# Source scores of layer 0 by GpSimd products and ScalarE sums, and a later place for some small GpSimd operations of layer 1

## The chip, the cores and the metric

The kernel runs on one core of a Trainium2 chip. The metric is the device time of one execution in microseconds (us). The core has a matrix engine (TensorE, PE in the profile; its weight loads are a row of their own, PEld), three engines for elementwise work (VectorE or DVE, ScalarE or ACT, GpSimd or POOL) and a queue engine (SyncE or SP) that issues transfers. The engines run side by side. Each takes its own instructions strictly in order and waits on semaphores for the others.

## The reference, cut to what matters

There are 3327 nodes with 256 features each, and a sparse 0/1 adjacency matrix with about four neighbours in a row. Two layers follow each other, each with a residual and a layer norm around it.

```python
# layer 0
Wh = h @ W
src = Wh @ a[:F_out]                 # one number per node
dst = Wh @ a[F_out:]
e = leaky_relu(src + dst.T, 0.2)
att = softmax(where(adj > 0, e, NEG_INF), axis=1)
h_prime = att @ Wh
...                                  # a GRU cell of h_prime and h
x = layernorm(x + gru)
# layer 1, two steps n = 0, 1; S is adj, R is (adj + I) by row sums
A  = top_p_attention(Xa, W1, W2, W3) # softmax row cut to its 0.9 nucleus, renormalised
Xf = R @ Xf
Xa = A @ Xa
Z  = Z + Xf @ U1[n].T + Xa @ U2[n].T
# after both steps
h = layernorm(X + Z) * ln_g + ln_b
x = layernorm(x + h)
```

The cut keeps, in a row of sorted probabilities, those whose preceding sum is below 0.9. Probabilities equal to the last one kept are ties, and how many of them stay depends on the order of their indices.

## The kernel before, in words

**Tiles and stages.** The 3327 rows make 26 tiles of 128 rows (the last has 127). In the profiled execution layer 0 lies from 0 to some 400 us, step 0 of layer 1 from there to about 930 us, and step 1 from there to the end. The orders of PE, ACT, DVE and POOL are written out by hand: each engine runs its instructions in the order in which the program text issues them. There is no planner.

**Start of layer 0** (`Layer0.run`). `weights()` makes two things out of W and the vector a: `by_a`, W times both halves of a laid along partitions (narrow PE products L813 and ACT copies L817), and `by_row`, W times the second half, repeated on all partitions (L822 to L824). Then tile groups are turned (`turn`, PE transposes and an ACT copy) and the destination scores are taken from x and `by_row` on DVE (`scores`, L855). The source scores come from PE: `project` (L872) multiplies the transposed tile by a column of `by_a`, 128x1 products, and ACT copies them to `ds` (L876).

**Loop of layer 0.** It runs in phases, six for each tile. In each phase DVE searches a part of an adjacency tile for its ones (`neighbours`, L935), and one to five tiles that are under way each go one step further in `tile(t)`: counts and offsets on ACT (`over1` L972 and after, `mid` L986, `tell` L988, `y` L990), a PE product that brings every edge its row's data (`pe` L1000), ACT's copies (`ei` L1004, `erow` L1005), DVE's choice of neighbour (`which` L1009 to `k` L1017), five gathers by POOL (L667), the weights and sums, and the GRU. `project` is called once before the loop for tiles 0 and 1 and once in each of the phases 3 to 26. `tell_src` (DVE, four small operations) splits source scores into the three parts that `pe` carries, at phases 1, 10 and 28 for tiles 0-1, 2-7 and 8-25. In phase 4 ACT issues the loads of the GRU's weights (L1217). From phase 13 on `gates_weights` multiplies them by W (PE L833, copies L838 on DVE and ACT), and at phases 8 and 10 `make_weights` prepares layer 1's weights (DVE copies L656 and L661).

**Step 1 of layer 1** (`Layer1.run`, the loop L2412 to L2481). Work item i of step 1 handles one tile of rows. Its stages are spread over several turns of the loop:

- three items ahead: logits (PE L1762) and the copy of them by ACT (L1765);
- two items ahead: the largest eight of each part of a row (DVE MAX8 L1778), the row's maximum, the exponentials (ACT L1860, and of the candidates L1872);
- one item ahead: a sorted list of the largest values (`list_1`), and `list_2`, which calls `settle` (L1802): DVE finds the threshold t and the number d of ties to drop, and POOL works out `lim` (L1822), `short` (L1824), `many` (L1826) and the flag (L1827) that tells whether the list was long enough. `gone` (POOL L1944 and L1945) lists the ties to drop. `mask` needs it: a match-replace over the whole row (DVE L1954, 3327 wide) drops these ties, and a whole-row product with a sum (L1924) keeps what is at least t;
- in the item's own turn: PE transposes the masked row block in seven groups (`turn` L2042, ACT copies L2044) and multiplies by the values (`times`, `pav` L2058). `one_over` (POOL L1933 and L1934) inverts the row sum to `rA`;
- after it: ACT scales the product by `rA` (`scaled`, L2066), POOL adds the neighbour term (L2067), and two layer norms follow in `tile_end` and `by_sums`. Each norm calls `sums`: an ACT sum (L2014), the negated mean `min` on POOL (L2016), an ACT sum of squares with that bias (L2019), three small POOL operations for scale and shift `mv` (L2021 to L2023), an ACT application (L2025). Between the norms POOL multiplies by `ln_g` (L2089) and adds x plus bias (L2091).

Two norms run at once: the second norm of an older tile (tags `bt`) and the first of a newer one (`at`). `propagate` computes R times the values from POOL's gathers (L667): PE L1983, ACT L1987, POOL add L1988. `put_aside_1` and `put_aside_2` store rows whose flag is set in a list of hard tiles: a flag cast on POOL (L2110), the PE product `pos` (L2113), small POOL operations (L2117 to L2127), an index on DVE (L2144) and POOL's `left_over` scatter (L2145). The hard tiles are treated again, with other methods, at the end.

**The order around the change.** `product(i, slots)` runs through the item's seven groups of PE work, and behind group g it calls the functions in `slots[g]`, in the order of their entry. That order decides where each engine's instructions stand. On POOL, one turn of the loop reads before the change: `left_over`, two gathers, `far` to `pay`, add L2067, the two `min` L2016, three gathers, `one_over`, `lim`, `short`, `many`, flag, `gone`, the six `mv`, add L1988, flag cast, product L2089, add L2091.

Of the kernel before, what the change touches and what calls it, by code (L numbers as in the profile page):

```python
# [16 lines left out]
P = 128  # L17
N = 3327
D = 256
# [694 lines left out]
class Layer0:  # L714
# [6 lines left out]
    def __init__(self, sh, ctx, adj, W, WT, a, wihT, whhT, b_ih, b_hh):  # L721
# [8 lines left out]
        self.by_a = keep.tile([P, DC, 2], F32, name="by_a")  # L730
        self.by_row = keep.tile([P, D], F32, name="by_row")
# [75 lines left out]
    def weights(self):  # L807

        nc = self.nc
        for c in range(DC):  # L810
            pa = self.ps.tile([P, 512], F32, tag="sm", name=f"pa{c}")
            for o in range(DC):
                nc.tensor.matmul(  # L813
                    pa[:, 0:2], self.WT_sb[:, o, c * P : (c + 1) * P], self.a_sb[:, o::DC],
                    start=(o == 0), stop=(o == DC - 1),
                )
            nc.scalar.copy(self.by_a[:, c, :], pa[:, 0:2])  # L817

        pr = self.ps.tile([P, 512], F32, tag="sm", name="pr")
        for o in range(DC):  # L820
            ab = self.work.tile([P, 2 * D], F32, tag="rz", name=f"ab{o}")[:, :P]
            nc.vector.tensor_scalar(ab, self.sh.ones, self.a_sb[:, DC + o : DC + o + 1], None, ALU.mult)  # L822
            nc.tensor.matmul(pr[:, :D], ab, self.WT_sb[:, o, :], start=(o == 0), stop=(o == DC - 1))
        nc.vector.tensor_copy(self.by_row, pr[:, :D])  # L824
# [24 lines left out]
    def scores(self, t0, t1):  # L849

        nc, sh = self.nc, self.sh
        for t in range(t0, t1):
            r = rows(t)
            junk = self.work.tile([P, 2 * D], F32, tag="rz", name=f"junk{t}")
            nc.vector.scalar_tensor_tensor(  # L855
                junk[:r, :D], sh.x1[:r, t, :], 1.0, self.by_row[:r], ALU.mult, ALU.mult,
                accum_out=sh.x1w[:r, t, self.DST : self.DST + 1],
            )
        if t1 < NT:
            nc.sync.dma_start(  # L860
                sh.whx[t0 * P : t1 * P, :].rearrange("(t p) w -> p t w", p=P), sh.x1w[:, t0:t1, :]
            )
        else:
            move_rows(nc.sync, sh.whx[t0 * P : N, :], sh.x1w[:r, t0, :], r)

    def project(self, t0, t1):

        nc, r = self.nc, rows(t1 - 1)
        pw = self.ps.tile([P, 512], F32, tag="sm", name=f"pw{t0}")[:, : t1 - t0]
        for t in range(t0, t1):  # L870
            for c in range(DC):
                nc.tensor.matmul(  # L872
                    pw[:r, t - t0 : t - t0 + 1], self.xT[:, c, cols(t)], self.by_a[:, c, 0:1],
                    start=(c == 0), stop=(c == DC - 1),
                )
        nc.scalar.copy(self.ds[:r, t0:t1], pw[:r])  # L876
# [270 lines left out]
    def run(self):  # L1147
# [38 lines left out]
        with self.tc.manual_schedule(engines=engines):  # L1186
# [13 lines left out]
            self.project(0, 2)  # L1200
            for _ in range(5):
                find()
            while phase < EVERY * NT or tiles:
                advance(FINDS[phase % EVERY])
                if phase == 1:
                    self.tell_src(0, 2)
                if 2 < phase <= NT:
                    self.project(phase - 1, phase)
                if phase == 10:
                    self.tell_src(2, 8)  # L1210
                if phase == NT + 2:
                    self.tell_src(8, NT)
                if phase in (8, 10):
                    next(qk_weights)
                if phase == LOAD_AT:
                    for w, src in ((self.plain, wih), (self.whh, whh)):
                        nc.scalar.dma_start(w, src.rearrange("(c p) d -> p c d", p=P))  # L1217
                if phase > 2 * EVERY:
                    next(gates, None)
# [19 lines left out]
class Layer1:  # L1239
# [562 lines left out]
    def settle(self, lst, before, last, thr2, r, drop, flag, tag, room=None):  # L1802
# [16 lines left out]
        )  # L1819
        lim = self.small("lim8", f"lim8{tag}")  # L1820
# [7 lines left out]
        return t, d, lim  # L1828
# [74 lines left out]
    def list_2(self, i):  # L1903

        nc, v = self.nc, self.items[i]
        n, r, tag = v.n, v.r, v.tag
        length = LIST[1]
        e = v.e[:r, :length]
        before = self.work.tile([P, length], F32, tag="before", name=f"before{tag}")
        nc.vector.tensor_tensor_scan(before[:r], e, e, 0.0, ALU.add, ALU.add)  # L1910
        v.t, v.d, v.lim = self.settle(
            v.lst, before[:r], v.last, v.thr2, r, DROP, self.flag[:r, n, v.at : v.at + 1], tag
        )

# [94 lines left out]
    def sums(self, h, r, tag):  # L2009
# [6 lines left out]
        nc.gpsimd.tensor_scalar(minus[:r], s[:r], -1.0 / D, None, ALU.mult)  # L2016
# [247 lines left out]
    def hard(self, k):  # L2264
# [20 lines left out]
        t, d, _ = self.settle(lst, before, last, thr2, P, HARD_DROP, flag, tag, room)  # L2285
# [98 lines left out]
    def run(self):  # L2384
# [5 lines left out]
        with self.tc.manual_schedule(engines=engines | {mybir.EngineType.Pool}):  # L2390
# [17 lines left out]
            self.gone(NT)  # L2408
            self.mask(NT)
# [3 lines left out]
            for i in range(NT, total):  # L2413
# [11 lines left out]
                slot(1, self.one_over, i)  # L2425
# [5 lines left out]
                if i + 1 < total:  # L2431
                    self.list_1(i + 1)
                    slot(1, self.list_2, i + 1)
                    slot(1, self.gone, i + 1)
                if i + 2 < total:
# [24 lines left out]
                for g in (0, 1, 2):  # L2460
                    slot(g, next, older, None)
# [136 lines left out]
```

## Time and profile before

| what | before |
|---|---|
| median of 3 runs | 1696.85 us (1692.40 to 1698.18) |
| profiled execution, its own time | 1693.33 us |
| its span | 1691.3 us |
| mean granted TensorE clock | 0.932 |
| POOL L667, gathers of layer 0, 130 | 1.04 us each |
| DVE L935, searches, 104 | 1.03 us each |
| POOL L2091, 26 adds | 3.58 us each |
| PE L2058, 1352 products | 0.40 us each |

A group line of the page names the source line, the engine, the operation, the output and input tiles, the count, the busy time, the mean in ns, and the idle time ahead of the group. A timeline line has the start and duration in us, the engine, the line, the operation, and in brackets the idle time ahead of it with what ended it. A wait line reads: engine, the tile and line that waited, what it waited for, then total us, how many times, the longest. A stretch line gives the stretch and its length, then for PE, its weight loads, DVE, ACT and POOL the busy time with the number of instructions, then the granted PE clock, the DMA share and GB/s.

### The profile page before, as it was taken

How to read it: one execution, taken by the hardware profiler on the slowest of the kernel's cores; microseconds unless marked ns; L12 is line 12 of the kernel's file. 1: busy time of each engine (PE TensorE's matmuls, PEld its weight loads, DVE VectorE, ACT ScalarE, POOL GpSimd, SP SyncE). 2: the span in 40 equal slices, each digit the busy share in tenths (PEclk: the TensorE clock that was granted, in tenths of full speed). 3: DMA queues.
4: the chain of work that ended last, by engine and by line, in shares of the span. 5: the costliest groups of instructions: out<-in, count | busy, mean ns of one | idle time of the engine just before them, and what ended most of it. 6: DMA issues, size and time to landing. Idle time of an engine off the chain costs nothing.

```text
span 1691.3 us, 27502 instructions
## 1 busy us (share of the span) xinstructions
PE 1457.9 (86%) x7899; PEld 980.9 (58%) x7899; DVE 1348.6 (80%) x4847; ACT 1080.6 (64%) x2631; POOL 1062.3 (63%) x1577
## 2 busy tenths in 40 slices
PE   4899999876999999999988799999999999875524
PEld 3766666544555555555554477776776666664413
DVE  5799999438877888887862999999998987875992
ACT  4478888646677777777753566666665676763511
POOL 0466666415566666666663468888888787778431
PEclk7599999987999999999999899999999999997766
DMA  8977775223344444434442112222222222211000
GB/s 256 332 261 257 256 256 131 75 79 95 102 116 110 111 123 113 109 109 114 115 119 58 35 54 72 68 57 72 67 68 70 64 63 63 60 53 33 19 6 5
DMA packets 101639, 178.75 MB, mean 106 GB/s; under 512 B 25977, under 2 KB 64119, under 8 KB 101479
## 3 DMA queue, kind: packets, MB, share of 16 engines
q0 software_dynamic: 26288, 73.68, 17.1%
q1 hardware_dynamic: 61818, 93.49, 17.0%
q10 hardware_dynamic: 13372, 9.74, 1.8%
q8 instruction: 65, 1.06, 0.3%
q14 instruction: 96, 0.78, 0.2%
HBM read 139.86 MB, written 37.06 MB: 105 GB/s over the span
## 4 chain that ended last, share of the span: by engine, by line
PE 41%; DVE 17%; POOL 14%; ACT 11%; issue 11%; DMA 6%; POOLq 0%; ACTq 0%; DVEq 0%; SPq 0%
PE pav L2058 11%; PE pl L1762 5%; POOL g L667 4%; DVE at L935 4%; DMA g<-x1k,uidx 3%; PE pav L1659 3%; PE pt L2042 3%; PE pxf L1983 2%; PE pc L1422 2%; POOL g L1598 2%; ACT at L2044 2%; PE pxf L1402 2%; PE plt L1634 2%; ACT p L1860 1%; ACT array L1765 1%
## 5 line engine op out<-in xcount | busy, mean ns | idle before, releaser
L2058 PE MATMUL pav<-xu,at 128*128 128x256 f32 (+2 forms) x1352 | 346.1, 399 | 35.6 <-ACT at L2044 35.6
L2058 PEld LDWEIGHTS pav<-xu,at 128*128 128x128 f32 (+2 forms) x1352 | 249.2, 195 | 135.0 <-ACT at L2044 63.3
L1778 DVE MAX8 cand<-array 128x8 f32<-128x104 f32 (+5 forms) x1233 | 260.3, 287 | 8.5 <-ACT array L1765 8.1
L1765 ACT COPY array<-pl 128x416 f32<-128x416 f32 (+3 forms) x402 | 184.5, 512 | 129.2 <-PE pl L1762 128.9
L1762 PE MATMUL pl<-kT,qT 64*128 64x416 f32 (+3 forms) x804 | 205.6, 569 | 8.7 <-ACT array L1765 7.6
L667 POOL DMA_INDIRECT g<-y_rows,edge x130 | 140.0, 1077 | 46.2 <-issue 33.8
L667 POOL DMA_INDIRECT g<-whx,edge x130 | 135.0, 1039 | 47.0 <-issue 37.3
L667 POOL DMA_INDIRECT g<-x_rows,edge x130 | 134.8, 1037 | 45.5 <-issue 30.8
L2044 ACT COPY at<-pt 128x512 f32<-128x512 f32 (+2 forms) x182 | 95.5, 543 | 99.6 <-PE pt L2042 99.4
L1598 POOL DMA_INDIRECT g<-x1k,uidx x130 | 136.4, 1049 | 34.5 <-issue 30.1
L1762 PEld LDWEIGHTS pl<-kT,qT 64*128 64x128 f32 (+1 forms) x804 | 67.2, 188 | 77.3 <-issue 56.8
L935 DVE FIND_INDEX8 at<-ones,array 128x8 uint32<-128x840 f32 (+1 forms) x104 | 105.9, 1027 | 0.0
L1698 POOL TENSOR_TENSOR x<-x,c 128x256 f32<-128x256 f32 (+1 forms) x26 | 26.8, 1032 | 109.5 <-ACT c L1693 109.5
L2091 POOL TENSOR_TENSOR h<-h 128x256 f32<-128x256 f32 (+1 forms) x26 | 93.2, 3584 | 2.0
L1666 DVE TENSOR_SCALAR rA<-pav 128x1 f32<-128x1 f32 (+1 forms) x26 | 4.1, 158 | 77.3 <-PE pav L1659 77.3
L1659 PE MATMUL pav<-g,w 128*128 128x257 f32 (+1 forms) x260 | 62.6, 388 | 3.4 <-DVE w L1653 3.4
L1052 PE MATMUL acc<-g,m 128*128 128x258 f32 (+1 forms) x260 | 63.2, 391 | 0.0
L1052 PEld LDWEIGHTS acc<-g,m 128*128 128x128 f32 (+1 forms) x260 | 50.7, 195 | 18.4 <-issue 7.7
L1983 PE MATMUL pxf<-g,m 128*128 128x256 f32 (+1 forms) x260 | 61.3, 383 | 0.0
L1079 PE MATMUL prz<-wih,hT 128*128 128x512 f32 (+1 forms) x104 | 51.8, 622 | 3.0 <-ACT hT L1072 1.1
L1659 PEld LDWEIGHTS pav<-g,w 128*128 128x128 f32 (+1 forms) x260 | 48.3, 193 | 10.4 <-DVE w L1653 3.8
L1886 DVE SCALAR_TENSOR_TENSOR cand<-ec,high 128x256 f32<-128x256 f32 (+1 forms) x104 | 51.4, 494 | 2.8
(556 smaller groups left out, 3830.0 us busy)
## 6 DMA issues: line engine op xcount, KB each, us to landing
array<-in_adj_dram SPq DMA_DIRECT2D x25, 1248.0 KB
array<-in_adj_dram SPq DMA_DIRECT2D x25, 415.5 KB
members<-m SPq DMA_DIRECT2D x26, 320.0 KB
m<-members SPq DMA_DIRECT2D x26, 320.0 KB
x_rows<-x ACTq DMA_DIRECT2D x25, 128.0 KB
x1k<-x ACTq DMA_DIRECT2D x25, 128.0 KB
xb_rows<-xb SPq DMA_DIRECT2D x25, 128.0 KB
y_rows<-y SPq DMA_DIRECT2D x25, 128.0 KB
```

The lines of the kernel that those rows point to most:

```text
L667: self.nc.gpsimd.indirect_dma_start(out=dst[:, b, :], out_offset=None, in_=table[:, :], in_offset=bass.IndirectOffsetOnAxis(ap=self.edge[: ...
L935: nc.vector.max_index(at[:r, g, :], self.ones8[:r], ad[:r, g, :])
L1052: nc.tensor.matmul(acc[:r, : self.WH], m[:, :r], g[:, k, :], start=(k == 0), stop=(k == EB - 1))
L1598: nc.gpsimd.indirect_dma_start(out=v.g2[:, b, :], out_offset=None, in_=sh.x1k[:, :], in_offset=bass.IndirectOffsetOnAxis(ap=v.idx[:, b : b ...
L1659: nc.tensor.matmul(v.acc[:r, : D + 1], v.w[:, b, :r], v.g2[:, b, : D + 1], start=(b == 0), stop=(b == UB - 1))
L1762: nc.tensor.matmul(pl[:r, :w], q[on], self.sh.kT[on, n, s : s + w], start=True, stop=True)
L1765: nc.scalar.copy(l[:r, h * HALF + s : h * HALF + s + w], pl[:r, :w])
L1778: self.nc.vector.max(cand[:r, g * 8 : g * 8 + 8], src[:r, g * group : min(N, (g + 1) * group)])
L1983: nc.tensor.matmul(acc[:r, :D], v.m[:, b, :r], v.g[:, b, :], start=(b == 0), stop=False)
L2044: nc.scalar.copy(at[:, :full, :r], pt[:, :full, :r])
L2058: nc.tensor.matmul(v.acc[: v.r, :D], at[:k, j - 4 * g, : v.r], V[:k, j, :], start=(j == 0), stop=(j == NT - 1))
L2091: nc.gpsimd.tensor_tensor(h, h, term, ALU.add)
```

## The change

In layer 0, `by_a` and `project` go. `by_row` now holds W times both halves of a, made by four pairs of a DVE operation and a PE product in one PSUM tile, and one copy. The source score of a tile is a product of x and `by_row` on POOL (`source_1`) and a sum over the row on ACT (`source_2`). The products of tiles 0 and 1 are issued ahead of the loop, and those of two further tiles in each of the phases 1 to 12; the sums stand at the head of the next phase on ACT. The tiles of products have two buffers. `tell_src` moves to phases 2, 8 and 15 (tiles 0-1, 2-11, 12-25), and `make_weights` to phases 18 and 20.

In step 1 of layer 1, `settle` becomes a generator that stops once t and d are known. Its last four operations run when `told` is called: at the head of slot 2 instead of inside `list_2` in slot 1 (for the last item right behind `gone`). `one_over` moves from the head of slot 1 to slot 2. The negated mean is computed by ACT. POOL's turn then reads: `left_over`, two gathers, `far` to `pay`, add L2067, three gathers, `gone`, the six `mv`, `lim`, `short`, `many`, flag, add L1988, flag cast, `one_over`, product L2089, add L2091.

```diff
-        self.by_a = keep.tile([P, DC, 2], F32, name="by_a")
-        self.by_row = keep.tile([P, D], F32, name="by_row")
+        self.by_row = keep.tile([P, 2, D], F32, name="by_row")
...
     def weights(self):
-        for c in range(DC):
-            pa = self.ps.tile([P, 512], F32, tag="sm", name=f"pa{c}")
+        pr = self.ps.tile([P, 2, D], F32, tag="sm", name="pr")
+        for k in (1, 0):
             for o in range(DC):
-                nc.tensor.matmul(
-                    pa[:, 0:2], self.WT_sb[:, o, c * P : (c + 1) * P], self.a_sb[:, o::DC],
-                    start=(o == 0), stop=(o == DC - 1),
-                )
-            nc.scalar.copy(self.by_a[:, c, :], pa[:, 0:2])
-
-        pr = self.ps.tile([P, 512], F32, tag="sm", name="pr")
-        for o in range(DC):
-            ab = self.work.tile([P, 2 * D], F32, tag="rz", name=f"ab{o}")[:, :P]
-            nc.vector.tensor_scalar(ab, self.sh.ones, self.a_sb[:, DC + o : DC + o + 1], None, ALU.mult)
-            nc.tensor.matmul(pr[:, :D], ab, self.WT_sb[:, o, :], start=(o == 0), stop=(o == DC - 1))
-        nc.vector.tensor_copy(self.by_row, pr[:, :D])
+                ab = self.work.tile([P, 2 * D], F32, tag="rz", name=f"ab{k}_{o}")[:, :P]
+                nc.vector.tensor_scalar(ab, self.sh.ones, self.a_sb[:, k * DC + o : k * DC + o + 1], None, ALU.mult)
+                nc.tensor.matmul(pr[:, k, :], ab, self.WT_sb[:, o, :], start=(o == 0), stop=(o == DC - 1))
+        nc.vector.tensor_copy(self.by_row, pr)
...
-    def project(self, t0, t1):
-
-        nc, r = self.nc, rows(t1 - 1)
-        pw = self.ps.tile([P, 512], F32, tag="sm", name=f"pw{t0}")[:, : t1 - t0]
-        for t in range(t0, t1):
-            for c in range(DC):
-                nc.tensor.matmul(
-                    pw[:r, t - t0 : t - t0 + 1], self.xT[:, c, cols(t)], self.by_a[:, c, 0:1],
-                    start=(c == 0), stop=(c == DC - 1),
-                )
-        nc.scalar.copy(self.ds[:r, t0:t1], pw[:r])
+    def source_1(self, t):
+
+        r = rows(t)
+        self.times_a[t] = m = self.work.tile([P, D], F32, tag="h", name=f"times_a{t}")
+        self.nc.gpsimd.tensor_tensor(m[:r], self.sh.x1[:r, t, :], self.by_row[:r, 0, :], ALU.mult)
+
+    def source_2(self, t):
+
+        r, m = rows(t), self.times_a.pop(t)
+        self.nc.scalar.activation(m[:r], m[:r], AF.Identity, accum_out=self.ds[:r, t : t + 1])
...
-            self.project(0, 2)
+            self.times_a = {}
+            self.source_1(0)
+            self.source_1(1)
...
-                if phase == 1:
+                for t in list(self.times_a):
+                    self.source_2(t)
+                if phase == 2:
                     self.tell_src(0, 2)
-                if 2 < phase <= NT:
-                    self.project(phase - 1, phase)
-                if phase == 10:
-                    self.tell_src(2, 8)
-                if phase == NT + 2:
-                    self.tell_src(8, NT)
-                if phase in (8, 10):
+                for t in (2 * phase, 2 * phase + 1):
+                    if t < NT:
+                        self.source_1(t)
+                if phase == 8:
+                    self.tell_src(2, 12)
+                if phase == NT // 2 + 2:
+                    self.tell_src(12, NT)
+                if phase in (18, 20):
                     next(qk_weights)
...
     def settle(self, lst, before, last, thr2, r, drop, flag, tag, room=None):
...
+        yield t, d
         lim = self.small("lim8", f"lim8{tag}")
...
-        return t, d, lim
+        yield lim
...
-        v.t, v.d, v.lim = self.settle(
+        v.settled = self.settle(
             v.lst, before[:r], v.last, v.thr2, r, DROP, self.flag[:r, n, v.at : v.at + 1], tag
         )
+        v.t, v.d = next(v.settled)
+
+    def told(self, i):
+        v = self.items[i]
+        v.lim = next(v.settled)
...
     def sums(self, h, r, tag):
...
-        nc.gpsimd.tensor_scalar(minus[:r], s[:r], -1.0 / D, None, ALU.mult)
+        nc.scalar.activation(minus[:r], s[:r], AF.Copy, scale=-1.0 / D)
...
             self.gone(NT)
+            self.told(NT)
             self.mask(NT)
...
-                slot(1, self.one_over, i)
                 slot(1, next, beside, None)
...
                     slot(1, self.gone, i + 1)
+                    if i + 2 == total:
+                        slot(1, self.told, i + 1)
...
                 for g in (0, 1, 2):
+                    if g == 2:
+                        slot(g, self.one_over, i)
+                    if g == 2 and i + 2 < total:
+                        slots[g].insert(0, lambda i=i: self.told(i + 1))
                     slot(g, next, older, None)
                     slot(g, next, last, None)
```

## The prediction

> **What bounds the kernel now.** I read the busy shares first, then busy time by stretch, then the waits of a stretch, and last the timeline of one period. The page:
>
> ```profile
> span 1691.3 us, 27502 instructions
> PE 1457.9 (86%) x7899; PEld 980.9 (58%) x7899; DVE 1348.6 (80%) x4847; ACT 1080.6 (64%) x2631; POOL 1062.3 (63%) x1577
> L2091 POOL TENSOR_TENSOR h<-h 128x256 f32<-128x256 f32 (+1 forms) x26 | 93.2, 3584 | 2.0
> ```
>
> No engine is full over the run. Step 1 of layer 1, the only part of layer 1 that is edited, runs from about 943 to 1691 us. By stretch (time, then busy time of each engine, PE clock last):
>
> ```profile
> 1043.00:1246.00 203.00, 195.05 (x972) 143.38 (x972) 188.97 (x640) 130.95 (x298) 168.30 (x289) 1.00 0.24 68
> 1381.00:1482.00 101.00, 89.99 (x433) 65.79 (x432) 84.03 (x284) 68.94 (x147) 76.44 (x137) 0.97 0.21 61
> 1482.00:1545.00 63.00, 48.59 (x232) 39.99 (x230) 44.79 (x117) 38.37 (x74) 51.36 (x96) 0.89 0.16 46
> ```
>
> In the steady stretch PE (96%) and DVE (93%) both lack only a little, so a shorter wait pays only until one of them is full. Later both have more air. The waits of the steady stretch (nine periods), total, count, longest:
>
> ```profile
> ACT h L2025 <- POOL mvbt L2023: 10.6, 9, 1.2
> PE pav L2058 <- ACT at L2044: 8.2, 18, 0.6
> DVE p L1954 <- POOL gone L1945: 4.1, 5, 0.8
> DVE array L1954 <- POOL gone L1945: 3.3, 4, 0.8
> ```
>
> All three engines stop once a period for a POOL result, or for ACT that stood waiting for POOL. One period on POOL and DVE:
>
> ```profile
> 1138.29 0.22 POOL L2016 TENSOR_SCALAR minbt<-sbt 128x1 f32<-128x1 f32 x1
> 1138.94 0.21 POOL L2016 TENSOR_SCALAR minat<-sat 128x1 f32<-128x1 f32 x1 [0.43 <-ACT junkat L2014]
> 1143.56 0.30 POOL L1933 TENSOR_SCALAR rA<-pay,sA 128x1 f32<-128x1 f32 x1
> 1144.53 0.29 POOL L1822 TENSOR_SCALAR lim<-last,e 128x1 f32<-128x1 f32 x1
> 1145.96 0.35 POOL L1944 TENSOR_SCALAR gone<-col,d 128x8 f32<-128x8 f32 x1
> 1146.40 0.34 POOL L1945 TENSOR_SCALAR gone<-gone,t 128x8 f32<-128x8 f32 x1
> 1150.71 4.06 POOL L2091 TENSOR_TENSOR h<-h 128x256 f32<-128x256 f32 x1
> ```
>
> ```profile
> 1146.77 0.09 DVE L1954 MATCH_VALUE_LOAD p<-gone,p 128x8 f32 x1 [0.82 <-POOL gone L1945]
> 1146.85 3.61 DVE L1954 MATCH_REPLACE8 p<-gone,p 128x3327 f32<-128x3327 f32 x1
> 1150.50 3.68 DVE L1924 SCALAR_TENSOR_TENSOR p<-p,t 128x3327 f32<-128x3327 f32 x1
> ```
>
> The loop that sets the 22.58 us period (1124.19, 1146.77, 1169.35) closes over POOL and DVE: `gone` releases the match-replace, the full-row product behind it (L1924) ends at 1154.18, the POOL add L2091, alone 0.72 us, is held until 0.59 us after that (4.06 us), and from there POOL works its list through, almost without a gap, to the next `gone`. That list lasts 15.17 us (22.58 less the 7.41 of the two DVE passes).
>
> **The change, step 1 of layer 1.** Three pieces leave POOL's list ahead of `gone`: the minus of the mean, 1138.31 to 1139.15 with its wait on ACT, 0.84 us; the two `one_over` operations, 1143.56 to 1144.53, 0.97; `lim`, `short`, `many` and `flag`, 1144.53 to 1145.96, 1.43. Together 3.24 us, and the list from L2091 to `gone` falls to 11.93. DVE's stall is only 0.82, so `gone` ceases to be last. What is late next: DVE's own work, 22.58 - 0.82 = 21.76, or PE's, 22.58 - 0.33 - 0.58 (its two stalls behind ACT copies L2044, which follow ACT's waits of 1.18 and 0.59 for `mvbt` and `mvat`; these come 3.24 us earlier too) = 21.67. So at most 0.8 to 0.9 a period.
>
> The postponed work is not gone. After `mvbt` and `mvat` (2.34 us behind `gone`) now come the four list operations, 1.43, and then the add L1988, 0.73, the flag cast, `one_over`, 0.97, the product L2089 and the add L2091. L1988 thus starts 3.77 us after `gone`; the product L1924 starts 3.73 after the match-replace. What POOL has not begun by then stands until it ends: L2091 4.06 for 0.72, and small POOL operations caught there last 3.3 to 3.5 us for 0.2 (L2016, L2124). Three cases. (1) `one_over` done in time: L2089 is held, L2091 ends 0.7 later than now, 8.7 us after the match-replace, and with 11.93 POOL needs 20.7 a period. (2) `one_over` held: 7.41 + 0.97 + 0.73 + 0.72 = 9.9, POOL 21.8. (3) L1988 held: 8.0 + 0.15 + 0.97 + 0.73 + 0.72 = 10.6, POOL 22.5, less the 0.57 that the first gather waits for PE today, 21.9; but `rA` is ready 9.1 after the match-replace, and ACT's L2066 wants it at 8.2 (1154.98). Behind that stand the copies L2044 of 1155.33, and PE's second stall grows from 0.58 to about 1.5. Gains of (1), (2), (3): 0.8, 0.7, about 0.1. As POOL has slack in (1), starts in it, and drifts towards (3) only as the held work eats the slack, I take 0.5 a period, ends 0 and 0.9.
>
> For ACT the minus is two 128x1 operations a period, 0.2 to 0.3 each (its 128x1 rows), beside idle time of 0.5 to 2.9 in the same period. No wait is added for POOL; ACT's Square no longer crosses to POOL and back.
>
> The Trainium skill, "SBUF — State Buffer", section "SBUF: two separate sides", says that VectorE and GpSimd share a port pair as an exclusive lock, and that a VectorE operation with two SBUF inputs shuts a reading GpSimd operation out for its whole length. The rows of L2091 agree (4.06 against 0.72, while L1988 keeps 0.73 beside the match-replace). Taken alone the rule speaks against pushing 2.4 us of POOL work towards L1924: by it case (3) is the lasting one and the steady stretch gains about 1 us instead of 6.
>
> Sum over the 26 items, by the starts of the match-replaces on DVE's timeline and the wait ahead of each. 1011 to 1282: 12 periods x 0.5 = 6 (0 to 11). 1282 to 1331: `gone` waits 4.25 and 0.99, PE follows closely: 2 (0 to 4). 1331 to 1381: periods of 25.1 that PE fills (stalls 0.3 and 0.6): 0.8 (0 to 2). 1381 to 1482: waits 3.78, 4.48, 3.83, 2.13, and PE stalls 2.24 each behind ACT: 5 of 14 (2 to 8). 1482 to 1545: periods of 28 and 17 with DVE stalled 6.30 for `gone`, POOL the busiest engine: 4 of the 4.4 by which `gone` advances (2 to 6). 1545 to 1691: DVE chain of the last tiles, not edited: 0. Together -17.8 (-4 to -31).
>
> **The change, layer 0.** Up to 34.3 us `weights()` has four pairs of ab and product in place of two pairs and four narrow products: two small DVE operations more, four PE products fewer: 0 (-0.3 to +0.3). After that PE loses 104 matmuls of some 0.35 us (a tile 0.87 to 1.03), POOL gets 26 products (0.65 to 0.73 alone, L2067, L1988; 1.03 in row L1698) and ACT 26 sums (0.51, as L2014) for 25 copies of 0.16. ACT is in order, so what is queued behind the sums matters: the weights' loads L1217, issued at 42.95 and 43.70, now wait for eight tiles' sums. With two product buffers POOL and ACT alternate at about 0.83 us a tile, so the loads go at about 45. `ei` L1004 (53.55) stands behind 24 sums and comes at about 60.4. Who waits:
>
> ```profile
> 58.30 0.69 DVE L838 COPY wih<-pm 128x512 f32<-128x512 f32 x1 [3.55 <-PE pm L833]
> 58.91 0.16 DVE L1009 TENSOR_TENSOR which<-place,ei 128x5 f32<-128x5 f32 x1
> 61.89 0.69 DVE L838 COPY wih<-pm 128x512 f32<-128x512 f32 x1 [1.54 <-PE pm L833]
> ```
>
> L1009 goes from 58.91 to about 60.6. The stalls ahead of L838 (3.55, 1.54) cover part: PE reaches the products earlier without its small matmuls. DVE's next searches start about 1.2 later (62.5 to 63.7), but all `tell_src` is then done (1.1 us, now at 79) and the weight copies moved to phases 18 and 20 (0.7) are still to come. From 73 to about 246 us DVE works without a gap, so the shift stays: +0.6 (-2 to +6, the upper end with products of 1.03 and no cover).
>
> The Trainium skill, "TensorE: Matmul & The Clock Gate", Part 1, says PE runs at half clock until it has been busy for some microseconds. The granted clock from 40 to 60 us is 0.50 to 0.60; by the rule, removing the small matmuls could keep it at half for the L833 products, which would cost about 1.8 us (first 3.7, second 1.96). I don't count it.
>
> Total -17.8 + 0.6 = -17.2. The profiled execution took 1693.33 (span 1691.3 and 2.0 around it), which gives 1676; it is 3.5 below the median of the three runs, 1696.85, from which it would be 1680. I say 1678, from the middle of the two, 1695, as I do for the rivals.
>
> **Rivals.** *Half the gain*: case (3) holds in the steady stretch, or the ACT passes of the last tiles keep PE late after 1381. For: the 0.04 us between 3.77 and 3.73. Against: POOL begins with 3.24 us of slack. 1 + 1 + 0.5 + 3 + 2 for the five stretches, less 0.6 = -7: 1688. *No change*: PE, at 96%, fills the period as soon as it is let, and layer 0 takes the late gain (+4): within 5 us, 1690 to 1700. For: waits come back elsewhere. Against: PE's own stalls are from the same POOL list. *Slower*: `rA` is late. If L1988 is held in most items (`gone` ending less than 0.1 us ahead of the match-replace is the point from which it decides), `rA` comes 0.9 us after ACT needs it, the copies L2044 and the two exp passes slip, and both PE and DVE wait about 0.6 more than today: 20 items x 0.6 = +12, and the late gain is eaten by the same delay: 1708. Against: a longer period gives POOL back its slack, so the delay corrects itself. *Layer 0 slow*: products of 1.03 as in row L1698 and nothing that covers: +6 in place of +0.6, -17.8 + 6 = -12, 1683. For: VectorE is busy beside them. Against: its rows there are mostly single-input searches L935.
>
> **How the numbers follow.** Full gain (-12 to -28) 0.48, more than that 0.05, half gain or a slow layer 0 (-5 to -12) 0.22, no change 0.11, slower 0.14. A measurement can tell 0.3%, about 5 us, from no change. So faster 0.75, same 0.11, slower 0.14. The range from 1665 to 1699 leaves about 0.05 below and 0.15 above; the likeliest case alone has 1668 to 1686.
>
> **What would show it.** Right: the DVE waits for `gone`, 43.4 us over the whole span (27.6 with `array`, 15.8 with `p` as the tile), fall below 12; ACT's L2025 waits for `mvbt` vanish; the match-replaces come 21.8 to 22.3 apart; the held 4 us moves from L2091 to L2089; the first `which` (L1009 today) comes at about 60.6. Wrong: new ACT waits for `rA` ahead of L2066, PE waits for `pos` on the flag cast, or `one_over` rows of 3 us mean that the postponed list fell under L1924; the source sums taking more than 0.9 us a tile mean a slow layer 0.

## The result and the profile after

The changed kernel takes 1674.37 us in the median of 5 runs (1668.83 to 1678.08), the kernel before 1697.11 us in the median of 5 (1692.40 to 1698.18). The ratio is 0.9867 with a 95% interval of 0.9842 to 0.9891: 22.7 us faster. The prediction said 1678 (1665 to 1699). The profiled execution took 1668.83 us with a span of 1667.0, so it is 5.5 us below the median of its kernel, as the one before was 3.8 below its own.

The page of the kernel after, the same lines as shown of before:

```profile
span 1667.0 us, 27301 instructions
PE 1427.8 (86%) x7791; PEld 956.5 (57%) x7791; DVE 1362.3 (82%) x4849; ACT 1100.7 (66%) x2710; POOL 1068.9 (64%) x1549
```

The steady stretch of step 1, again by stretch (time, busy time of PE, its weight loads, DVE, ACT, POOL, then the clock):

```profile
1043.00:1246.00 203.00, 198.61 (x995) 148.09 (x994) 196.29 (x672) 137.03 (x322) 167.71 (x276) 1.00 0.25 72
```

DVE's share of it rose from 188.97 to 196.29 us: almost full. The waits of the same stretch:

```profile
POOL mvbt L2022 <- ACT junkbt L2020: 8.1, 10, 1.6
ACT junkat L2015 <- POOL h L2068: 2.9, 9, 0.3
PE pav L2059 <- ACT at L2045: 2.6, 9, 0.3
```

No wait of DVE for `gone` is left there, none of ACT for `mvbt`, and PE's wait for the copies fell from 8.2 to 2.6. POOL still waits for ACT, but at `mvbt`, which now stands behind `gone`. One period on POOL:

```profile
1134.22 0.33 POOL L1946 TENSOR_SCALAR gone<-gone,t 128x8 f32<-128x8 f32 x1
1135.25 0.19 POOL L2022 TENSOR_SCALAR mvbt<-sqbt 128x1 f32<-128x1 f32 x1 [0.71 <-ACT junkbt L2020]
1138.62 0.29 POOL L1823 TENSOR_SCALAR flag<-many,short 128x1 f32<-128x1 f32 x1
1140.25 0.57 POOL L1935 TENSOR_TENSOR rA<-rA,minus_one 128x1 f32<-128x1 f32 x1
1140.79 0.73 POOL L2090 TENSOR_TENSOR h<-h,ln_g 128x256 f32<-128x256 f32 x1
1141.60 3.99 POOL L2092 TENSOR_TENSOR h<-h 128x256 f32<-128x256 f32 x1
```

And on DVE, where the match-replace starts without a wait:

```profile
1137.37 0.08 DVE L1955 MATCH_VALUE_LOAD p<-gone,p 128x8 f32 x1
1137.44 3.61 DVE L1955 MATCH_REPLACE8 p<-gone,p 128x3327 f32<-128x3327 f32 x1
1141.08 3.92 DVE L1925 SCALAR_TENSOR_TENSOR p<-p,t 128x3327 f32<-128x3327 f32 x1
```

`gone` is done at 1134.55, 2.8 us ahead of the match-replace. All that was postponed ends before DVE's product; the add L2092 is held under it as before (3.99 us). Over the whole span DVE waits 5.4 us for `gone`, where it waited 43.4 before. The period is 21.9 us (1115.47, 1137.37, 1159.34) in place of 22.58.

Where the time went, by the starts of the match-replaces (before, after, what the piece gained):

| piece | before | after | gain |
|---|---|---|---|
| start to the first match-replace (layer 0, step 0) | 943.54 | 938.21 | 5.3 |
| first to fourth | 67.8 | 66.8 | 0.9 |
| 12 steady periods | 270.9 | 264.0 | 6.9 |
| next 2 (waits 4.25 and 0.99) | 48.8 | 45.9 | 2.9 |
| next 2 | 50.2 | 46.7 | 3.5 |
| next 4 | 101.2 | 95.0 | 6.1 |
| last 2 | 45.1 | 43.7 | 1.4 |
| last match-replace to the end | 163.9 | 166.6 | -2.7 |

### The profile page after: what moved, and what is told of

Same layout as the page of the kernel before. It is cut to its first block, busy times and chain, and to the rows that moved or that the text cites. A ratio compares the mean times of both kernels' runs of the same rounds, so it can differ in the third digit from the quotient of the medians.

```text
span 1667.0 us, 27301 instructions
## 1 busy us (share of the span) xinstructions
PE 1427.8 (86%) x7791; PEld 956.5 (57%) x7791; DVE 1362.3 (82%) x4849; ACT 1100.7 (66%) x2710; POOL 1068.9 (64%) x1549
## 3 DMA queue, kind: packets, MB, share of 16 engines
q8 instruction: 64, 1.05, 0.3%
## 4 chain that ended last, share of the span: by engine, by line
PE 48%; DVE 16%; POOL 13%; issue 10%; ACT 7%; DMA 4%; ACTq 0%; POOLq 0%; DVEq 0%; SPq 0%
PE pav L2059 16%; PE pl L1757 6%; POOL g L667 4%; DVE at L925 4%; PE pt L2043 3%; PE pxf L1984 3%; DMA g<-x1k,uidx 3%; POOL g L1593 2%; PE pav L1654 2%; PE pc L1417 2%; PE pxf L1397 2%; PE plt L1629 1%; DVE array L1961 1%; PE pu L1569 1%; ACT array L1504 1%
## 5 line engine op out<-in xcount | busy, mean ns | idle before, releaser
L2059 PE MATMUL pav<-xu,at 128*128 128x256 f32 (+2 forms) x1352 | 339.4, 396 | 21.9 <-ACT at L2045 21.9
L1042 PEld LDWEIGHTS acc<-g,m 128*128 128x128 f32 (+1 forms) x260 | 50.5, 195 | 22.3 <-issue 7.7
L1882 DVE SCALAR_TENSOR_TENSOR cand<-ec,high 128x256 f32<-128x256 f32 (+1 forms) x104 | 56.4, 543 | 2.8
L2092 POOL TENSOR_TENSOR h<-h 128x256 f32<-128x256 f32 (+1 forms) x26 | 55.3, 2129 | 2.0
```

The lines of the kernel that those rows point to most:

```text
L1042: nc.tensor.matmul(acc[:r, : self.WH], m[:, :r], g[:, k, :], start=(k == 0), stop=(k == EB - 1))
L1882: nc.vector.scalar_tensor_tensor(v.cand[:r], ec[:r], high[:r, j : j + 1], ec[:r], ALU.is_ge, ALU.mult, accum_out=above[:r, j : j + 1])
L2059: nc.tensor.matmul(v.acc[: v.r, :D], at[:k, j - 4 * g, : v.r], V[:k, j, :], start=(j == 0), stop=(j == NT - 1))
```

## Experiments: each part alone

Layer 0 and step 1 apart, and each of the three pieces of step 1 alone.

**Layer 0 alone**: the hunks of `weights`, `source_1`, `source_2` and the loop of layer 0 as in the diff of the change, and nothing of layer 1.

```diff
-            self.project(0, 2)
+            self.times_a = {}
+            self.source_1(0)
+            self.source_1(1)
```

> Only the part of layer 0 is changed. Theory A (from the trace after: DVE's first search 1.3 us later, search 17 3.5 later, search 78 2.4 later, and nothing that gives it back): the run is 1 to 3 us slower than before, ratio 1.0006 to 1.002, with the searches as late as in the trace after. Theory B (the first match-replace of step 1 came 5.3 us earlier after the change, because layer 0 passes on less PE work): 3 to 6 us faster, ratio 0.9965 to 0.998, and the first match-replace of step 1 near 938 us. Theory C: what is late in layer 0 is absorbed by waits behind 290 us: 0, within 1 us.

Measured: 1689.78 us against 1693.73, ratio 0.9968 (0.9950 to 0.9986). **Step 1 alone**: the hunks from `settle` on, and nothing of layer 0.

```diff
-        return t, d, lim
+        yield lim
...
-                slot(1, self.one_over, i)
```

> Only the part of step 1 is changed. Theory A: the whole gain is here, 22 to 26 us, ratio 0.985 to 0.987, at least as fast as the whole change; match-replaces 21.9 us apart in the steady stretch. Theory B: 17 to 19 us, ratio 0.989 to 0.990, as layer 0 brought 5 of the 23.

Measured: 1675.81 us, ratio 0.9898 (0.9878 to 0.9919). So theory B holds for both: the layer 0 of the change is worth 2 to 8 us by the interval of its ratio, and is not a loss. **The negated mean alone:**

```diff
-        nc.gpsimd.tensor_scalar(minus[:r], s[:r], -1.0 / D, None, ALU.mult)
+        nc.scalar.activation(minus[:r], s[:r], AF.Copy, scale=-1.0 / D)
```

> Only the negated mean goes to ACT: 0.84 of the 3.24 us leave POOL's list ahead of the mask. Theory A (the list need only fall by DVE's stall of 0.8; what is beyond that pays only in the last items): steady periods of 22.58 fall to 21.95 to 22.0, 7 us, and each of the nine late waits by up to 0.84, 5 to 7 us: 12 to 14 us faster, ratio 0.992 to 0.993. Rival B (the gain goes with the work that leaves the list): 0.84 / 3.24 of 21.6 us, 5.6 us, ratio 0.9967. Rival C (ACT is as near its limit as DVE and pays for two more operations): no change, steady period 22.5 or more.

Measured: 1669.57 us, ratio 0.9864 (0.9844 to 0.9884). One line brings the whole of the gain, more than even theory A gave it. The steady period is 21.7, and of the nine late waits for `gone` three are left, 1.37, 1.53 and 1.49 us. **The four list operations alone**: `settle` as a generator and `told` as in the change, with `one_over` and the negated mean as before.

```diff
+                    if g == 2 and i + 2 < total:
+                        slots[g].insert(0, lambda i=i: self.told(i + 1))
                     slot(g, next, older, None)
```

> Only the four list operations are postponed behind the list of ties and the mv operations: 1.43 of the 3.24 us leave POOL's list ahead of the mask, and the add in front of the flag cast starts later by as much. Theory A: steady periods of 21.9 to 22.0 (7 us), late waits down by up to 1.4 each (8 to 11): 15 to 18 us faster, ratio 0.9895 to 0.991. Rival B (in proportion): 9.5 us, ratio 0.9944. Rival C (the add or the flag cast is caught under the whole-row product of DVE, as the start of the add is 3.77 us behind the list of ties and the product 3.73 behind the match-replace): the steady period stays above 22.3, the gain is under 8 us, and the add L1988 of before shows rows of 4 us.

Measured: 1690.56 us, ratio 0.9978 (0.9962 to 0.9994). Rival C comes nearest, though it is the flag cast and not the add that is caught. POOL of this kernel, one period:

```profile
1177.85 0.29 POOL L1828 TENSOR_SCALAR flag<-many,short 128x1 f32<-128x1 f32 x1
1178.10 0.64 POOL L1994 TENSOR_TENSOR h<-h,x 128x256 f32<-128x256 f32 x1
1178.68 3.58 POOL L2116 CAST flag<-flag 128x1 bf16<-128x1 f32 x1
1182.23 0.72 POOL L2095 TENSOR_TENSOR h<-h,ln_g 128x256 f32<-128x256 f32 x1
1183.03 0.79 POOL L2097 TENSOR_TENSOR h<-h 128x256 f32<-128x256 f32 x1
```

The match-replace began at 1174.46. The 1.43 us taken from the front of `gone` pushed the flag cast under DVE's product (3.58 us for 0.19), so that L2095 and L2097, 1.5 us, are both done behind the product. Before, L2089 was done ahead of it, and L2091 ended 0.59 us behind it. What that costs is seen on DVE, in the same period:

```profile
1178.18 4.04 DVE L1930 SCALAR_TENSOR_TENSOR array<-array,t 128x3327 f32<-128x3327 f32 x1
1182.56 0.67 DVE L1887 SCALAR_TENSOR_TENSOR cand<-ec,high 128x256 f32<-128x256 f32 x1
1183.28 0.82 DVE L1887 SCALAR_TENSOR_TENSOR cand<-ec,high 128x256 f32<-128x256 f32 x1
```

The last two in the kernel before, behind the product of 3.68 us:

```profile
1154.53 0.52 DVE L1886 SCALAR_TENSOR_TENSOR cand<-ec,high 128x256 f32<-128x256 f32 x1
1155.10 0.48 DVE L1886 SCALAR_TENSOR_TENSOR cand<-ec,high 128x256 f32<-128x256 f32 x1
```

DVE hardly waits for `gone` any more: in the twelve steady periods 2.35 us once and at most 0.45 otherwise. But its product, which starts beside POOL's add L1994, and the two operations beside L2095 and L2097 are together 0.85 us longer, as much as the wait of 0.82 that is gone. The period is 22.3 to 22.7, in two of the twelve 24.77 and 23.54 (in the longer one `left_over` waits 2.62 us for DVE): nothing won there. **`one_over` alone**:

```diff
-                slot(1, self.one_over, i)
...
                 for g in (0, 1, 2):
+                    if g == 2:
+                        slot(g, self.one_over, i)
                     slot(g, next, older, None)
```

> Only the inverse of the row sum is moved; POOL still waits for ACT's sums. Theory A (with that wait in place POOL is late, so the moved pair is caught under DVE's whole-row product, as the flag cast was with the list operations alone, and comes back on POOL's list): steady period 22.3 or more, ratio 0.997 to 1.004. Rival B (0.97 us off the list pays like 0.84 off it by the negated mean): period 21.7 to 21.9, ratio 0.986 to 0.990.

Measured: 1688.69 us, ratio 0.9971 (0.9958 to 0.9984), steady period 22.3, one of the twelve 24.77 with the same wait of `left_over`. Theory A, with another operation caught than it named: `rA` gets through, and the product L2089 is held.

```profile
1175.52 0.56 POOL L1934 TENSOR_TENSOR rA<-rA,minus_one 128x1 f32<-128x1 f32 x1
1176.05 3.88 POOL L2089 TENSOR_TENSOR h<-h,ln_g 128x256 f32<-128x256 f32 x1
1180.00 0.79 POOL L2091 TENSOR_TENSOR h<-h 128x256 f32<-128x256 f32 x1
```

Outside the long period DVE's wait for `gone` falls from 0.82 to between 0.10 and 0.24 us, and of what that gives 0.34 is lost again in one of DVE's operations, beside L2091 (0.82 us for 0.48).

The parts give 0.22%, 0.29% and 1.36%; the three together 1.02% (0.81 to 1.22). They don't add, and the largest is the one with the least work in it.

## Experiments: is it POOL's work or POOL's wait

The negated mean is 0.43 us of work in two operations, and a wait of 0.43 us for ACT's sum. Two kernels take these apart. Both have the negated mean on ACT and a spare operation on POOL in the old place, whose output nothing reads. The first reads a constant, the second ACT's sum:

```diff
+        spare = self.st.tile([P, 1], F32, tag="spare" + tag[0], name=f"spare{tag}", bufs=2)
+        nc.gpsimd.tensor_scalar(spare[:r], self.power[:r], -1.0 / D, None, ALU.mult)   # first kernel
+        nc.gpsimd.tensor_scalar(spare[:r], s[:r], -1.0 / D, None, ALU.mult)            # second kernel
```

> As the negated mean on ACT, but POOL still does an operation of the same kind and size in the same place, on a constant: its work is back, its wait for ACT's sum is not. The result of it is used by nothing. Theory A (what POOL lost was the wait for ACT, 0.43 in the steady stretch and up to 3.2 in the last items, not the 0.4 of work): 17 to 22 us faster, ratio 0.987 to 0.990, late waits of the match-replace for the list of ties as with the negated mean alone. Rival B (the work): half of the 0.84 is back, steady period 22.2 or more, gain 8 to 12, ratio 0.993 to 0.995.

> As the one before, but the spare operation on POOL reads ACT's sum: POOL's work and its wait are both back, while ACT still makes the negated mean for itself. Theory A (POOL's wait in the queue ahead of the list of ties is the cost): time and waits of before, ratio 0.997 to 1.000, steady period 22.5. Rival C (the gain is on ACT, whose sum of squares no longer waits for POOL): ratio 0.986 to 0.989, as with the negated mean alone.

Measured: with the work and no wait 1670.89 us, ratio 0.9860 (0.9831 to 0.9890); with work and wait 1695.43 us, ratio 1.0016 (0.9996 to 1.0036). Theory A in both. The waits of the kernel whose spare operation reads the sum, in the steady stretch:

```profile
ACT h L2027 <- POOL mvbt L2025: 10.6, 9, 1.2
PE pav L2060 <- ACT at L2046: 8.3, 18, 0.6
DVE p L1954 <- POOL gone L1945: 4.2, 5, 0.8
POOL spareat L2018 <- ACT junkat L2014: 3.9, 9, 0.4
DVE array L1954 <- POOL gone L1945: 3.4, 4, 0.9
```

They are the waits of before, to a tenth. The kernel with the constant has none of them but

```profile
PE pav L2060 <- ACT at L2046: 2.6, 9, 0.3
```

So the 0.43 us for which POOL stood behind ACT set the period, and what ACT gains by making its own bias is worth nothing by itself. How 0.43 us can bring 0.87 a period was not tried; the traces show it in the operation of POOL which the product catches. In the kernel with the negated mean alone:

```profile
1159.99 0.34 POOL L1945 TENSOR_SCALAR gone<-gone,t 128x8 f32<-128x8 f32 x1
1164.15 0.73 POOL L2089 TENSOR_TENSOR h<-h,ln_g 128x256 f32<-128x256 f32 x1 [0.71 <-ACT h L2025]
1164.96 0.72 POOL L2091 TENSOR_TENSOR h<-h 128x256 f32<-128x256 f32 x1
1165.85 4.31 POOL L2145 DMA_INDIRECT left_over<-pay,idx  x1 [0.17 <-issue]
```

DVE's product runs there from 1165.37. Before, L2091 began at 1150.71 and the product at 1150.50: the add missed the start by 0.2 us and ended 0.59 after the product. A few tenths earlier, and the add is done ahead of it; what is held is the scatter `left_over`. From the end of DVE's product to the end of the next `gone` POOL then takes 12.9 us (from 1169.17 to one period of 21.7 behind 1160.33) in place of 15.1 (from 1154.18 to one period of 22.58 behind 1146.74).

## Experiments: what the other two pieces do beside the negated mean

The edits of the kernels with one piece alone are put together in pairs: the line of the negated mean with the hunks of `told`, and the same line with those of `one_over`.

```diff
+        nc.scalar.activation(minus[:r], s[:r], AF.Copy, scale=-1.0 / D)    # both
+                        slots[g].insert(0, lambda i=i: self.told(i + 1))   # first kernel
+                        slot(g, self.one_over, i)                          # second kernel
```

> The negated mean on ACT and the four list operations postponed; the inverse of the row sum stays ahead of the list of ties. Theory A (postponing is worth nothing once POOL does not wait for ACT ahead of the mask, and does no harm as POOL is then early): as the negated mean alone within 0.2%, ratio 0.985 to 0.988, steady period 21.7 to 21.95. Rival B (postponing does harm by itself, as alone, where the flag cast was held 3.6 us under DVE's whole-row product): steady period 22.3 or more, ratio 0.990 to 0.994.

> The negated mean on ACT and the inverse of the row sum moved behind the flag cast; the four list operations stay ahead of the list of ties. Theory A (the moved inverse is what makes the three pieces together worse than the negated mean with the list operations, by delaying POOL's product L2089 into the start of DVE's whole-row product): steady period 21.9, ratio 0.988 to 0.991, as the three pieces. Rival B (it is harmless): 21.7, ratio 0.985 to 0.9865.

Measured: with the list operations 1669.46 us, ratio 0.9849 (0.9821 to 0.9877); with `one_over` 1671.17 us, ratio 0.9868 (0.9846 to 0.9890). The steady periods are 21.6 to 22.2 and mostly about 21.7. Beside the negated mean each piece is worth nothing, and neither does harm: theory A of the first holds, rival B of the second. The period of 21.9 comes only with all three, where L2090 begins just ahead of DVE's product (1140.79 and 1141.08). Seven of these products take 3.84 to 3.94 us each, against 3.68 or 3.69 with the negated mean and `one_over`: that is about the difference of the two periods, and it makes 2.6 us in twelve of them. Step 1 alone and the negated mean alone lie 6 us apart in their medians; where the rest of that comes from is not shown.

**Layer 0 with the negated mean only**: all hunks of the change in layer 0, and of those in step 1 only this one:

```diff
-        nc.gpsimd.tensor_scalar(minus[:r], s[:r], -1.0 / D, None, ALU.mult)
+        nc.scalar.activation(minus[:r], s[:r], AF.Copy, scale=-1.0 / D)
```

> The part of layer 0 and the negated mean on ACT, nothing else: the four list operations and the inverse of the row sum stay where they were before. Theory A (the two gains are independent): 0.9864 x 0.9968 = 0.9833, 1665 us, faster than the whole change. Rival B (what layer 0 brought is one of the chances of step 0 and does not add): 0.986 to 0.987, 1670 us, as the whole change.

Measured: 1664.50 us (1660.54 to 1667.84, 6 runs), ratio 0.9817 (0.9788 to 0.9846). It beats both kernels in the median, the changed one by 10 us, though the intervals of the two ratios (0.9842 to 0.9891 there) overlap a little. The gains of layer 0 and of the negated mean add, as theory A says; its 0.9833 lies in the interval, the 0.986 of rival B does not.

## Experiments: layer 0

The trace after shows two costs in layer 0 that were not foreseen. Destination scores on DVE:

```profile
12.59 0.42 DVE L846 SCALAR_TENSOR_TENSOR junk<-x,by_row 128x256 f32<-128x256 f32 x1
12.94 0.94 DVE L846 SCALAR_TENSOR_TENSOR junk<-x,by_row 128x256 f32<-128x256 f32 x1
13.81 0.85 DVE L846 SCALAR_TENSOR_TENSOR junk<-x,by_row 128x256 f32<-128x256 f32 x1
49.92 0.22 DVE L881 CAST tell<-ds 128x10 bf16<-128x10 f32 x1 [1.78 <-ACT times_a L866]
59.43 0.66 DVE L999 TENSOR_TENSOR which<-place,ei 128x5 f32<-128x5 f32 x1 [1.28 <-ACT ei L994]
65.01 0.69 DVE L829 COPY wih<-pm 128x512 f32<-128x512 f32 x1 [2.80 <-PE pm L824]
```

POOL's first two products (12.64 to 14.38) run beside the second and third score. To see whether they cause the 0.94 and 0.85, the copy of `by_row`'s first half is put behind the scores:

```diff
-        nc.vector.tensor_copy(self.by_row, pr)
+        nc.vector.tensor_copy(self.by_row[:, 1, :], pr[:, 1, :])
+        self.pr = pr
...
         nc.vector.tensor_reduce(m, sh.x1w[:, :, self.DST], AX.X, ALU.max)
+        nc.vector.tensor_copy(self.by_row[:, 0, :], self.pr[:, 0, :])
```

> The part of layer 0 and the negated mean on ACT, with the copy of by_row's first half put behind DVE's scores, so that POOL's first two products no longer run beside the scores. Theory A (these two products cost DVE the 0.53 and 0.44 us by which the second and third score take 0.94 and 0.85 in place of 0.41): all 26 scores take 0.41, the first search starts 0.5 to 1 us earlier from the first score on than with the layer 0 of the change; the time is that of the two parts without it less up to 1, ratio 0.981 to 0.982. Rival B (the long scores have another cause): two scores stay at 0.85 or more.

Measured: every score takes 0.42, so POOL's products were the cause, as theory A says. But nothing is won by it, against the second half of theory A: from the first score to the first search pass 22.2 us, against 23.2 in the trace after and 22.0 in that of layer 0 with the negated mean, which has the two long scores too. DVE waits behind its scores for PE anyway (7.75 us at 31.08 in the trace after), and the long scores lie ahead of that wait. The time is 1667.00 us, ratio 0.9840 (0.9814 to 0.9865), no different from 0.9788 to 0.9846.

The other question is where layer 0 gains. The first match-replace of step 1 starts at 938.2 to 941.9 us in the four traces with the new layer 0 (mean 940.1) and at 938.5 to 950.1 in the nine with the old one, the kernel shown last here left aside (mean 944.5). At the first `rA` of step 0 the means are 448.7 and 449.6. So layer 0 itself brings about 1 us, and 3.4 arise in step 0, whose code is the same. These are means of few traces that scatter: from that `rA` to the match-replace the new ones take 490.4 to 492.5 us, the old ones 490.2 to 499.7. One row there differs between all the old and all the new, POOL's gather at 553 us. With the old layer 0 (kernel before):

```profile
550.89 1.00 POOL L1598 DMA_INDIRECT g<-x1k,uidx  x1 [0.81 <-issue]
553.14 1.88 POOL L667 DMA_INDIRECT g<-x_rows,edge  x1 [0.27 <-issue]
```

With the new (layer 0 alone):

```profile
549.40 1.00 POOL L1593 DMA_INDIRECT g<-x1k,uidx  x1 [0.45 <-issue]
551.65 1.05 POOL L667 DMA_INDIRECT g<-x_rows,edge  x1 [0.27 <-issue]
```

To test whether POOL's 26 new instructions move that, they are added to the kernel before, with nothing that reads them:

```diff
+                for t in (2 * phase - 2, 2 * phase - 1):
+                    if t < NT:
+                        m = self.work.tile([P, D], F32, tag="h", name=f"spare{t}")
+                        nc.gpsimd.tensor_tensor(m[: rows(t)], sh.x1[: rows(t), t, :], self.by_row[: rows(t)], ALU.mult)
```

> The kernel before, with 26 products of 128x256 added on POOL at the start of layer 0, two a phase, read by nobody; PE still makes the source scores. Theory A (step 0 of layer 1 gained with the new layer 0 because POOL's instructions stand elsewhere: the gather of x_rows that takes 1.88 us at about 553 in every kernel with the old layer 0 takes 1.05 in every one with the new): the slow gather there is gone, items 4 to 6 of step 0 take 59.2 us in place of 61, and the run is 2 to 5 us faster, ratio 0.997 to 0.999. Rival B (the cause lies with PE, ACT, addresses or queues): the gather at 553 still takes 1.88, ratio 0.9995 to 1.001.

Measured: the slow gather is gone, as theory A says (1.05 us at 553.74; the gather behind it takes 1.30). The median is 1692.01 us against 1695.34, but eight of the twelve runs lie at 1690.6 to 1692.6 and four at 1697.8 to 1698.8, and the ratio is 1.0004 (0.9988 to 1.0020), as rival B says. Items 4 to 6 take 59.9 us, between the two, and in this trace step 0 takes 491.2 us from its first `rA` to the match-replace, as with the new layer 0. So 26 more instructions on POOL are enough to move the slow gather, and by the interval they are worth 2 us at most. The test is not a clean one: nothing holds the spare products back, ten of them run in one stretch beside DVE's scores, and ten scores take 0.85 to 0.96 us. What of the new layer 0 speeds up step 0 stays open.

## Why the prediction was right, and where its steps were not

- **The loop that sets the period** was read rightly: `gone`, match-replace, DVE's product, the held add, POOL's list. With `gone` early, DVE's own work was next, at 21.9 where the prediction had 21.76 and, with drift, 22.1. The 21.76 took DVE's operations as they were; its product grew by 0.2 us. Twelve periods gave 6.9 us, the prediction took 6.
- **The 3.24 us as one sum of three pieces** is the step that failed, though the number came out. It counted work in front of `gone`; what mattered was the wait inside the first piece. The negated mean alone, 0.84 of the 3.24, brings 1.36%, and the other 2.4 us bring 0.2 to 0.3% each alone and nothing beside it. The prediction saw that only DVE's stall of 0.82 could be won, but not that one piece was enough for all of it.
- **Case (3)**, the postponed list held under DVE's product, was given as about 0.1 us a period; the kernel with only the list operations shows something like it, with the cast held for 3.58 us and not L1988: 22.3 to 22.7 in place of 22.58. But there it is DVE that pays, with 0.85 us on its own operations, which the prediction put at nothing. In the whole change the case did not come; `gone` is 2.8 us early there. The forecast that the held 4 us would move to L2089 was wrong: L2092 is still the one.
- **The late items**: 14 us against 12 predicted. That the sum is so near is luck, as two errors cancel. The two periods from 1331 on gave 3.5 for 0.8 predicted: PE was read as filling them, but DVE waited 3.35 and 3.31 for `gone` there, and one fell from 25.09 to 21.94. The last two gave 1.4 for 4 predicted. The tail, put at 0, lost 2.7; over all traces it is between 163.9 and 168.9 us long, and its cause was not tried.
- **Layer 0** had the wrong sign: +0.6 predicted, 2 to 8 us gained. The steps inside it were near: the loads at 45.33 (predicted 45), the first `which` at 59.43 (60.6), products of 0.72 us; search 17 is later by 3.5 us after the change and by 0.6 in the trace of layer 0 alone. What was left out were the two long scores, which cost nothing, the wait of 1.78 for the source sums of tiles 2 to 11, and above all that step 0 behind it moves by several us, for a reason that stays open.
- **The rule of the Trainium skill against the change**, the lock of "SBUF — State Buffer", section "SBUF: two separate sides", by which whoever starts first keeps the ports, agrees with the rows: operations of POOL caught by DVE's product took 3.6 to 4.3 us, and DVE took 0.94 for 0.42 in a score beside POOL's product and 3.92 for 3.68 in a whole-row product that starts just behind one. Case (3) did not become the lasting one for all that: who waits follows from the lock, but whether it matters followed from POOL's slack.
- **The clock rule**, "TensorE: Matmul & The Clock Gate", Part 1 in the Trainium skill, that was weighed and not counted: after the change the granted clock from 60 to 70 us is 0.66 (0.74 before). The second L824 group runs at 0.50 (62 to 66 us) and takes 5.47 us, and DVE waits 2.80 for it where it waited 1.54: 1.3 us of the 1.8 named, in this trace. In the one with layer 0 alone the clock is 1.00 (60 to 63 us), the group takes 2.83, and DVE waits 1.20.

## What to carry to other kernels

A small operation on an in-order engine can cost its wait more than its length: look at what stands behind it in the queue. Here two operations of 0.2 us that waited 0.43 us for another engine were worth more than 2.4 us of work without a wait. And where a long VectorE operation with two SBUF inputs holds GpSimd up, as for 3.6 to 4.3 us here, count what GpSimd finishes before it starts, and what it then runs beside VectorE's next operations. Moving work from one side to the other can gain nothing: with the list operations alone VectorE's operations grew by as much as its wait fell. So what a piece gains alone says little about its size.

## What the runs showed of the hardware that was not expected

A scatter issued by POOL is held by DVE's product as the arithmetic is: 4.31 us for `left_over` where it takes 1.1 otherwise. And step 0 of layer 1, the same instructions in every kernel, varied by several us. Around 880 to 890 us two traces with the same instructions up to there had these stretches, the first from step 1 alone, the second from the negated mean alone:

```profile
880.00:890.00 10.00, 8.05 (x56) 5.17 (x55) 4.58 (x16) 2.84 (x9) 7.55 (x8) 0.80 0.51 131
```

```profile
880.00:890.00 10.00, 8.40 (x70) 5.41 (x69) 4.62 (x16) 2.18 (x8) 7.98 (x9) 1.00 0.50 130
```

The item that lies there takes 16.8 us in the first and 13.5 in the second. PE's wait for the gathered rows differs by 0.35 us (1.21 and 0.86). In the first the wait ends at 886.61, and the granted clock is 1.00 up to 885 us and 0.50 from 886 to 892; in the second it stays at 1.00. The products behind come 3.3 us later in the first, ten times the difference of the waits. That the longer wait is what lowered the clock is likely from the order of the rows, but it was not tried. It is one part of the spread by which the first match-replace of step 1 starts anywhere between 938 and 950 us.
